# Encoder layers 0 to 4: the turned rows copied by VectorE, a new order of the steps, and new places for the last layer's end

## The chip, the core and the metric

The kernel runs on one NeuronCore of a Trainium2 chip. The metric is the device time of one execution in microseconds (us). Five engines work side by side, each through its own queue in order: PE (TensorE, matmuls; PEld is its weight loads), DVE (VectorE), ACT (ScalarE), POOL (GpSimd) and SP (SyncE, which here only issues DMAs). Engines wait for each other through semaphores.

## The reference, cut to what matters

Eight sequences of 256 rows with 128 features go through an encoder of six layers, a routed mixture of experts, a state-space block and two layers of local attention. The change touches the encoder's order, and the end of its last layer, where routing begins. One layer computes, for each sequence `h` (16 heads of 8, `rel` a fixed table that decays with the distance of two rows):

```python
q = (h @ wq.T + bq_).reshape(bh, sl, H, DH)
k = (h @ wk.T + bk_).reshape(bh, sl, H, DH)
scores = jnp.einsum('blhd,bmhd->bhlm', q, k) * inv_sqrt_d
w_avg = jax.nn.softmax(scores, axis=-1).mean(axis=1)
new_w = jax.nn.softmax(CSCALE * w_avg + rel[None], axis=-1)
sa = jnp.einsum('blm,bme->ble', new_w, h)
h1 = _ln(h + sa, l1w, l1b)
h2 = _ln(h1, l2w, l2b)
ff = jax.nn.relu(h2 @ w1.T + b1_) @ w2.T + b2_
return (_ln(h2 + ff, l3w, l3b), None)
```

After the six layers each row is normalized again and sent to one of eight experts; a shared expert takes every row.

## The kernel before, in words

**One block.** `plan(n, l, b)` (L450) lists the steps of one sequence b in one layer l; with six layers and eight sequences there are 48 such blocks, numbered n. Each step is a small function, and almost each belongs to one engine.

- `f_transpose` (PE, L463) turns the block's rows into `pt`; `f_copy` (ACT, L468) copies them to `ht`; `f_qk` (PE, L473 and L474) makes queries and keys in `pqk`; `f_bias` (DVE, L479 and L483) adds the biases and writes `qt`, `kt`; `f_mask` (POOL, L490) spreads the queries over masked copies `qm`.
- Scores come in four portions k of 64 rows and all 16 heads. `s_matmul k` (PE, L502) writes four tiles `s` of one PSUM bank each. For each of the four, `s_max k,g` (DVE, L512) takes the negated maxima and `s_exp k,g` (ACT, L516) two exponentials with their sums. `s_weights k` (DVE, L523) inverts the sums, `s_diag k` (POOL, L529) makes the diagonal weights `dg`.
- `mix c` (PE, L548, with the `rel` table at L546) adds the weighted heads of two portions up in `pacc`; `mix_exp c` (ACT, L558) is the second softmax's exponential, `nw`.
- `r_transpose` (PE, L567) and `r_copy` (DVE, L574) turn it; `r_mix` (PE, L581) applies it to the rows (`psa`); `r_add` (DVE, L590) adds the input and takes the first statistics (L426, L428); `rs1` and `r_norm1` (POOL: L274, L275, L444, L446, L280, L281) normalize to `t1`; `mv2` (DVE) takes the second statistics of `t1`, `rs2` and `r_norm2` (POOL) give `n2`, `r_residual` (POOL) `h2`.
- `r_transpose2` (PE, L615, `pt2`), `r_h2t` (DVE, L621), `r_ff10`, `r_ff11` (PE, L630, two `pf` tiles), `r_relu0` (ACT, L638), `r_relu1` (DVE, L640), `r_ff2` (PE, L646, `po`), `r_add3` (DVE, L654, with the third statistics), `rs3` and `r_norm3` (POOL) end the block.

**The order.** Nothing is scheduled by the compiler: each step has a place, in units of which a block has 16 (`SLOTS`), and block n starts at 16 n. All steps of all blocks are sorted by place and issued in that order, so each engine's queue is a weave of some six blocks in flight. The table `ORDER0` (L56) gives the places of layers 0 to 5; the last layer's sequences 3 to 7 have their own (`ORDER_END`, L74), its first three two changed entries (`LAST_NORM`, L188). `ORDER_ROUTE` (L152) places the routing of each sequence, `ORDER_SHARED` the shared expert, `BLOCKS` the routed experts' blocks.

```python
places = dict(ORDER0)
if l == DEPTH0 - 1 and b < 3:
    places.update(LAST_NORM)
elif l == DEPTH0 - 1:
    places = {name: at_b[b - 3] for name, at_b in ORDER_END.items()}
for name, fn, *args in steps:
    at(t0 + places[name], 0, lambda fn=fn, args=args: fn(*args))
```

**PSUM.** Six banks hold the `s` tiles (pool `ps_s`), so a portion of scores needs four banks that earlier exponentials have freed. The other two (pool `ps_m`) are shared by all else, ten tiles a block: `pt`, `pqk`, two `pacc`, `pnw`, `psa`, `pt2`, two `pf` and `po`. A tile's first matmul waits until the last reader of the bank's earlier tile is through.

**Around it.** `begin(b)` (L1029) normalizes the inputs of sequences 2 to 7 during the first blocks: statistics on DVE at place 3, the root on POOL at 5, the norm (L439) on DVE at 7. `state_space_weights` (L342) prepares weights for the later state-space block: on DVE a product over 128 x 1024 elements (L343), two copies of matmul results (L348), six small operations and eight fills, besides two matmuls, one exponential on ACT and one operation on POOL. It is issued once, at place 0.9 of block 8. In the last layer `route(b)` (L731) follows each sequence: norm, scores against the experts, choice, count, and two indirect DMAs on POOL (`send`, L825) that put the rows into the experts' buckets in HBM. `shared(q)` (L954) fits the shared expert in, and `block(j)` (L893) runs the 23 routed blocks after the last sequence.

Of the kernel before, what the change touches and what calls it, by code (L numbers as in the profile page):

```python
# [20 lines left out]
NB = 8  # L21
# [5 lines left out]
DEPTH0, HEADS0, DH0, FF0 = 6, 16, 8, 512  # L27
# [43 lines left out]
    "r_residual": 43.970, "r_ff2": 47.854, "r_add3": 50.870, "rs3": 59.957, "r_norm3": 73.951,  # L71
}

ORDER_END = {  # L74
    "f_transpose": (-22.588, -32.173, -31.874, -30.172, -34.750),
    "f_copy": (-21.688, -28.101, -28.555, -30.061, -31.562),
    "f_qk": (-15.007, -14.534, -23.086, -25.006, -11.950),
    "f_bias": (-11.801, -11.122, -22.761, -24.492, -11.386),
    "f_mask": (-6.524, -10.118, -9.553, -23.037, -10.705),
    "s_matmul0": (-1.917, -5.386, -4.976, -5.351, -2.724),  # L80
    "s_max0,1": (2.491, -1.850, -1.900, -1.396, -2.178),
    "s_max0,3": (-0.598, -2.685, -2.563, -4.623, -1.493),
    "s_max0,2": (2.064, -3.816, -1.374, 0.741, -0.178),
    "s_max0,0": (-0.500, -5.197, -3.092, -1.337, 0.111),
    "s_matmul1": (0.455, -4.912, -1.171, 0.708, 0.699),
    "s_max1,1": (3.047, -0.531, 1.568, 3.437, 2.386),
    "s_max1,3": (3.715, 2.999, 2.222, 2.638, 3.004),
    "s_max1,2": (3.231, -0.595, 2.205, 4.177, 3.024),
    "s_exp0,1": (3.643, -0.138, 0.483, -0.479, 4.027),
    "s_exp0,3": (0.851, -0.871, -0.805, 3.613, 4.500),  # L90
    "s_exp0,2": (3.180, -1.967, 1.421, 3.653, 5.676),
    "s_max1,0": (2.933, 0.569, 0.828, 3.343, 5.828),
    "s_exp0,0": (3.833, -2.528, -1.820, 1.700, 6.048),
    "s_matmul2": (5.225, 3.710, 1.519, 5.869, 6.113),
    "s_exp1,1": (4.254, 1.863, 1.976, 7.266, 6.121),
    "s_max2,2": (7.022, 4.300, 3.235, 9.812, 6.177),
    "s_max2,1": (5.683, 4.167, 4.387, 6.760, 6.819),
    "s_exp1,2": (6.460, 4.018, 2.497, 6.731, 7.639),
    "s_exp1,3": (5.773, 4.652, 2.319, 4.655, 7.897),
    "s_max2,3": (7.766, 5.905, 3.987, 7.528, 8.871),  # L100
    "s_exp1,0": (4.977, 3.283, 2.260, 7.101, 9.300),
    "s_max2,0": (6.315, 3.903, 3.011, 6.704, 9.322),
    "s_matmul3": (5.866, 5.622, 5.985, 7.454, 10.567),
    "s_exp2,3": (8.315, 8.107, 4.093, 9.815, 10.922),
    "s_exp2,2": (7.901, 7.763, 10.214, 10.035, 11.881),
    "s_weights1": (7.083, 6.767, 4.000, 9.885, 12.232),
    "s_weights0": (5.023, 2.985, 2.289, 7.492, 12.314),
    "s_exp2,0": (6.779, 5.030, 3.941, 7.395, 12.361),
    "s_exp2,1": (8.070, 7.574, 5.917, 8.060, 13.131),
    "s_max3,3": (8.729, 7.394, 11.437, 11.234, 13.794),  # L110
    "s_diag1": (9.827, 7.569, 7.357, 13.446, 14.625),
    "s_max3,2": (8.914, 10.690, 8.657, 10.503, 14.655),
    "s_weights2": (12.301, 15.947, 11.372, 12.768, 15.139),
    "s_diag0": (10.155, 11.733, 11.924, 12.185, 15.190),
    "s_exp3,3": (12.942, 10.368, 12.722, 13.062, 15.414),
    "s_max3,1": (7.821, 7.839, 7.230, 11.469, 16.156),
    "s_max3,0": (9.108, 7.588, 10.909, 12.174, 16.730),
    "mix0,0": (10.634, 12.537, 13.066, 14.510, 16.836),
# [12 lines left out]
    "r_copy": (24.987, 22.101, 26.159, 25.133, 25.460),
    "r_mix": (25.267, 24.231, 26.620, 26.265, 26.786),
    "r_add": (26.976, 25.221, 27.964, 26.481, 28.335),
    "rs1": (30.053, 28.735, 30.060, 27.687, 30.032),
    "r_norm1": (32.011, 30.898, 30.735, 32.891, 31.789),
    "mv2": (33.807, 32.685, 33.080, 34.231, 32.467),
    "rs2": (33.862, 34.167, 36.446, 35.913, 34.021),
    "r_norm2": (34.544, 36.241, 38.935, 36.012, 34.183),
    "r_transpose2": (37.022, 38.395, 39.134, 36.759, 35.411),
    "r_h2t": (38.682, 39.571, 40.982, 37.883, 36.035),  # L140
    "r_ff10": (42.293, 39.711, 42.076, 41.248, 36.086),
    "r_ff11": (44.071, 42.631, 44.347, 39.613, 36.743),
    "r_relu0": (43.173, 42.325, 44.133, 42.663, 37.228),
    "r_residual": (37.554, 45.597, 48.811, 47.127, 38.283),
    "r_relu1": (45.180, 45.140, 47.469, 41.160, 39.470),
    "r_ff2": (47.776, 52.122, 48.822, 44.199, 40.517),
    "r_add3": (49.717, 53.375, 50.144, 51.436, 41.812),
    "rs3": (52.100, 58.307, 50.265, 54.792, 43.345),
    "r_norm3": (52.128, 58.358, 53.988, 55.107, 43.817),
}  # L150

ORDER_ROUTE = {  # L152
    "stats": (57.612, 57.612, 57.612, 56.949, 58.400, 58.211, 56.128, 44.295),
    "scale": (60.894, 60.894, 60.894, 58.836, 58.984, 59.878, 56.249, 46.526),
    "norm": (62.335, 62.335, 62.335, 58.860, 62.344, 61.253, 58.677, 46.756),
    "turn": (62.504, 62.504, 62.504, 59.248, 63.854, 63.551, 59.091, 49.402),
    "turned": (63.254, 63.254, 63.254, 59.889, 67.055, 64.640, 59.917, 49.954),
    "score": (66.190, 66.190, 66.190, 64.538, 67.765, 66.095, 60.974, 51.586),
    "choose": (68.024, 68.024, 68.024, 65.682, 70.485, 70.473, 62.519, 51.710),
    "count": (68.716, 68.716, 68.716, 82.004, 71.716, 71.394, 64.683, 52.398),  # L160
    "decay": (70.616, 70.616, 70.616, 82.508, 71.081, 72.041, 63.836, 52.978),
    "gate": (76.085, 76.085, 76.085, 85.702, 78.182, 72.642, 64.451, 53.425),
    "weigh": (81.070, 81.070, 81.070, 86.757, 80.354, 73.182, 68.517, 54.034),
    "put": (70.108, 70.108, 70.108, 83.767, 80.866, 71.724, 67.600, 54.198),
    "send0": (83.835, 83.835, 83.835, 87.737, 83.795, 75.315, 69.536, 54.498),
    "send1": (83.933, 83.933, 83.933, 90.820, 87.761, 78.188, 69.998, 55.144),
}

ORDER_SHARED = {
    "up0": (12.819, 27.640, 35.497, 51.662),  # L170
    "up1": (33.023, 18.085, 43.056, 54.937),
    "up2": (55.700, 45.285, 35.385, 55.168),
    "silu0": (28.073, 32.749, 39.789, 55.600),
    "silu1": (33.768, 26.049, 45.482, 55.800),
    "silu2": (56.300, 55.400, 35.761, 55.900),
    "times1": (38.457, 42.862, 46.381, 56.000),
    "times0": (30.812, 34.798, 41.496, 56.600),
    "times2": (56.500, 56.100, 42.000, 56.800),
    "down0": (37.783, 56.200, 43.645, 57.100),
    "down1": (41.724, 57.000, 47.596, 57.200),  # L180
    "down2": (56.700, 57.300, 50.240, 57.600),
    "out": (56.900, 57.500, 55.500, 57.900),
    "turn": (57.400, 57.800, 56.400, 58.000),
    "add": (57.700, 58.100, 58.300, 58.200),
}

TABLE, REGISTERS, BLOCKS = 55.100, 55.200, 62.400
LAST_NORM = {"rs3": 51.325, "r_norm3": 53.252}  # L188


ORDER1 = {
# [56 lines left out]
def model_kernel(ctx: ExitStack, tc: tile.TileContext, A: dict, out: bass.AP):  # L248
    nc = tc.nc
# [111 lines left out]
    with ExitStack() as s0:  # L361
# [54 lines left out]
        SLOTS = 16  # L416
        slots = {}

        def at(slot, order, fn):
            slots.setdefault(round(slot + order / 10, 3), []).append(fn)  # L420
# [29 lines left out]
        def plan(n, l, b):  # L450
            t0 = SLOTS * n
            v = {}
# [12 lines left out]

            def f_copy():
                v["ht"] = wk.tile([P, T], F32, name="ht", tag="ht")
                nc.scalar.copy(v["ht"], v["pt"].rearrange("p n t -> p (n t)"))  # L468

            def f_qk():  # L470
                wa = v["w"][0]
# [213 lines left out]
                    steps += [(f"s_max{k},{g}", s_max, k, g), (f"s_exp{k},{g}", s_exp, k, g)]  # L685
            for c in range(NC):
                steps += [(f"mix{c},0", mix, c, 0), (f"mix{c},1", mix, c, 1), (f"mix_exp{c}", mix_exp, c)]
            places = dict(ORDER0)
            if l == DEPTH0 - 1 and b < 3:
                places.update(LAST_NORM)  # L690
            elif l == DEPTH0 - 1:
                places = {name: at_b[b - 3] for name, at_b in ORDER_END.items()}
            for name, fn, *args in steps:
# [317 lines left out]
            block(j, e1 + j)  # L1011
        at(e1 + 4, 9, where)

        at(SLOTS * NB, 9, lambda: state_space_weights(small_bank))
        for b in range(NB):
            at(
                SLOTS * (2 * NB + b) + 1, 0,
# [481 lines left out]
    with ExitStack() as s3:  # L1499
# [19 lines left out]
        SLOTS = 16  # L1519
# [346 lines left out]
        for n in range(DEPTH1 * NB):  # L1866
            l, b = n // NB, n % NB
# [114 lines left out]
```

## Time and profile before

| what | us |
|---|---|
| three runs | 1673.78, 1679.32, 1689.04; median 1679.32 |
| the profiled execution | 1682.49 |
| its span | 1680.6 |
| busy in the span: PE, DVE, ACT, POOL | 1527.3, 1411.0, 1287.0, 1184.7 |
| encoder layers 0 to 4, then the last layer to the routed experts | about 0 to 720, then to 910 |
| rest: routed experts, state space, local attention | 910 to 1680.6 |

The profiled execution is one of its own, 3.2 us above the median of the three runs; its span leaves out 1.9 us around the program. A line of a timeline gives the start and the length in us, the engine, the source line, the operation, the tile it writes and those it reads, their sizes and how many equal instructions were merged; in brackets the idle time before it and who ended it. A record can begin before its turn, while the one ahead of it is still running, so what an instruction takes of its queue is read from one start to the next. The grants of PE's clock stand as PEclk, 1.00 being full speed.

### The profile page before, as it was taken

Reading aid. Unit: us, or ns where it says so; the run is one execution under the profiler, and the core shown is the slowest. Engines: PE = TensorE matmul, PEld = TensorE weight load, DVE = VectorE, ACT = ScalarE, POOL = GpSimd, SP = SyncE. Lnnn points to the kernel's source line nnn. Section 1 sums busy time; section 2 is a strip of 40 time slices with the busy share of each in tenths; the row PEclk is TensorE's granted clock in tenths of the full one; section 3 lists DMA queues with packets and bytes.
Section 4 is the critical chain, followed back from the end, with each engine's and each line's share of the span. In section 5 each row is a group of like instructions: output and inputs, shape, how many; then the busy total and the mean of one; then the engine's idle time right before and its main releaser. Section 6 shows DMA issues by size and latency. Waiting matters only on the chain.

```text
span 1680.6 us, 37534 instructions
## 1 busy us (share of the span) xinstructions
PE 1527.3 (91%) x12864; PEld 918.9 (55%) x12880; DVE 1411.0 (84%) x3344; ACT 1287.0 (77%) x4593; POOL 1184.7 (70%) x1703
## 2 busy tenths in 40 slices
PE   7899999999999999999898868898986889999996
PEld 3565666666666666666664643232221555666664
DVE  5899899999999999998776437999897889888884
ACT  6898999999999999997661328775631677888873
POOL 3587888999888888888874026977864656666661
PEclk9999999999999999999899979999777999999997
DMA  4000064000000000000000320000000000000000
GB/s 116 2 2 2 18 205 139 18 12 2 4 27 2 2 19 11 2 2 1 8 8 21 111 56 11 1 0 1 1 0 1 1 2 1 1 2 1 8 7 13
DMA packets 43356, 35.36 MB, mean 21 GB/s; under 512 B 3973, under 2 KB 39327, under 8 KB 43167
## 3 DMA queue, kind: packets, MB, share of 16 engines
q1 hardware_dynamic: 40991, 30.10, 5.9%
q0 software_dynamic: 1024, 2.10, 0.4%
q8 instruction: 104, 1.70, 0.4%
q10 hardware_dynamic: 1152, 0.76, 0.2%
q14 instruction: 85, 0.70, 0.1%
HBM read 20.50 MB, written 12.45 MB: 20 GB/s over the span
## 4 chain that ended last, share of the span: by engine, by line
ACT 39%; PE 33%; DVE 20%; POOL 4%; issue 3%; DMA 1%; SPq 0%; DVEq 0%; POOLq 0%; ACTq 0%
ACT e L516 30%; PE s L502 4%; DVE h L1362 4%; PE pm L1444 3%; PE pacc L548 3%; PE pq L1586 2%; PE pm L1240 2%; DVE pm L1356 2%; ACT el L1693 2%; PE pe L913 2%; ACT r L638 1%; ACT nw L558 1%; PE sl L1670 1%; PE pte L1711 1%; DVE nm L1681 1%
## 5 line engine op out<-in xcount | busy, mean ns | idle before, releaser
L516 ACT ACTIVATE e<-s,nmax 128x256 f32<-128x256 f32 x1536 | 713.7, 498 | 39.0 <-DVE nmax L512 31.1
L512 DVE TENSOR_REDUCE nmax<-s 128x2 f32<-128x512 f32 x768 | 491.8, 677 | 69.8 <-PE s L502 65.1
L516 ACT ACTIVATION_READ_ACCUMULATOR e<-s,nmax 128x1 f32 x1536 | 354.1, 231 | 0.0
L502 PE MATMUL s<-kt,qm 32*128 32x256 f32 x3072 | 268.9, 413 | 8.7 <-ACT e L516 5.4
L502 PEld LDWEIGHTS s<-kt,qm 32*128 32x128 f32 x3072 | 160.7, 188 | 90.0 <-ACT e L516 56.2
L548 PE MATMUL pacc<-e,dg 128*32 128x256 f32 x3072 | 191.7, 390 | 2.2 <-DVE t L654 1.8
L1369 POOL TENSOR_TENSOR hc<-h,bc 128x1024 f32<-128x1024 f32 x64 | 150.4, 2356 | 60.2 <-DVE h L1362 55.7
L1362 DVE TENSOR_TENSOR_SCAN h<-da,pm 128x1024 f32<-128x1024 f32 x64 | 146.3, 2285 | 7.7
L1348 ACT ACTIVATE da<-pm,na 128x510 f32<-128x510 f32 x128 | 82.0, 682 | 86.5 <-PE pm L1444 86.0
L275 POOL TENSOR_TENSOR rs<-rs,mhalf 128x2 f32<-128x2 f32 x184 | 131.5, 715 | 15.3
L1693 ACT ACTIVATE el<-sl,nm,rn 128x128 f32<-128x128 f32 x256 | 114.4, 471 | 27.7 <-DVE nm L1684 27.7
L529 POOL TENSOR_TENSOR dg<-sel,z 128x256 f32<-128x256 f32 x192 | 116.3, 615 | 26.4 <-DVE z L523 25.4
L548 PEld LDWEIGHTS pacc<-e,dg 128*32 128x32 f32 x3072 | 91.4, 111 | 77.6 <-issue 18.2
L630 PE MATMUL pf<-h2t,wa 128*128 128x256 f32 x384 | 109.6, 409 | 24.7 <-DVE h2t L621 20.8
L1706 POOL TENSOR_TENSOR el<-el,rz 128x512 f32<-128x512 f32 x64 | 66.5, 1040 | 92.0 <-DVE rz L1701 92.0
L1444 PE MATMUL pm<-dt,ssel 32*128 32x512 f32 x256 | 114.3, 726 | 7.3 <-ACT da L1348 7.1
L274 POOL TENSOR_SCALAR rs<-mv 128x2 f32<-128x2 f32 x184 | 42.1, 229 | 111.5 <-DVE mv L428 49.3
L1444 PE MATMUL pm<-u,ssel 32*128 32x512 f32 x256 | 96.4, 751 | 17.4 <-DVE h L1362 17.4
L1586 PE MATMUL pq<-wqkv,y 128*128 128x512 f32 x192 | 98.3, 607 | 2.6 <-DVE hk L1541 1.8
L630 PEld LDWEIGHTS pf<-h2t,wa 128*128 128x128 f32 x384 | 66.6, 192 | 59.5 <-DVE h2t L621 31.0
L490 POOL TENSOR_TENSOR qm<-qt,kmask 128x1024 f32<-128x1024 f32 x48 | 90.9, 1893 | 8.7 <-DVE qt L479 8.7
L646 PE MATMUL po<-wf,r 128*128 128x128 f32 x768 | 95.5, 278 | 0.5 <-ACT xnt L759 0.5
(308 smaller groups left out, 3462.1 us busy)
## 6 DMA issues: line engine op xcount, KB each, us to landing
bucket<-zrow SPq DMA_DIRECT2D x1, 8640.0 KB, 28.8
ln<-in_ln_dram SPq DMA_DIRECT2D x6, 448.0 KB, 4.6
wa<-in_wa_dram SPq DMA_DIRECT2D x6, 384.0 KB, 3.0
wf<-in_wf_dram SPq DMA_DIRECT2D x6, 256.0 KB, 3.7
wqkv<-in_wqkv_dram SPq DMA_DIRECT2D x1, 1536.0 KB, 7.7
xb<-bucket SPq DMA_DIRECT2D x23, 64.0 KB, 1.8
routed<-ob SPq DMA_DIRECT2D x23, 64.0 KB, 1.6
w<-in_w1e_dram SPq DMA_DIRECT2D x1, 1408.0 KB, 32.4
```

Of the source, the lines that this page charges most:

```text
L275: nc.gpsimd.tensor_tensor(dst, dst, mhalf.to_broadcast(list(dst.shape)), ALU.pow)
L502: nc.tensor.matmul(ss[g][:, i, :], v["qm"][rows, 2 * k + i].rearrange("p j q -> p (j q)"), v["kt"][rows, :], start=True, stop=True,)
L512: nc.vector.tensor_reduce(v["nmax", k][:, g, :], v["s", k][g], AX.X, ALU.max, negate=True)
L516: nc.scalar.activation(v["e", k][:, g, i, :], v["s", k][g][:, i, :], AF.Exp, bias=v["nmax", k][:, g, i : i + 1], accum_out=v["z", k][:, g, ...
L529: nc.gpsimd.tensor_tensor(dg, sel32.unsqueeze(1).to_broadcast(sh), z.unsqueeze(2).to_broadcast(sh), ALU.mult)
L548: nc.tensor.matmul(acc, v["dg", k][:, 2 * g + i, :], v["e", k][:, g, i, :], start=(g == 0), stop=False,)
L630: nc.tensor.matmul(pf[:, i, :], v["w"][0][:, f0 : f0 + P], v["h2t"], start=True, stop=True)
L1362: nc.vector.tensor_tensor_scan(h.rearrange("p h t -> p (h t)"), da, pu.rearrange("p h t -> p (h t)"), 0.0, ALU.mult, ALU.add)
L1369: nc.gpsimd.tensor_tensor(hc, v["h", n], v["bc", 1].unsqueeze(1).to_broadcast([P, 2, T2]), ALU.mult)
L1444: nc.tensor.matmul(dst, ssel[rows, j, :], pairs[n // NU][src][rows, f, :], start=True, stop=True)
L1586: nc.tensor.matmul(pq, yb[:, col : col + P], wqkv[:, l, i * INNER : (i + 1) * INNER], start=True, stop=True)
L1693: nc.scalar.activation(v["e", c][:, par, j, :], v["s", c][par][:, j, :], AF.Exp, scale=v["rn", c][:, 0, h : h + 1], bias=v["nm", c][:, par ...
```

## The change

There are three parts. In layers 0 to 4 `f_copy` runs on VectorE; in layer 5 it stays on ScalarE. Layers 0 to 4 get their own table of places, `ORDER0_MID`; the first three sequences of the last layer keep `ORDER0`. All entries of `ORDER_END`, `ORDER_ROUTE` and `ORDER_SHARED` are new, and `state_space_weights` moves by half a block. No step is added or left out, and no tile changes.

On the queues the order of layers 0 to 4 becomes, with the block that holds scores k=0 to 3 (before | after, PE):

```
before: s0, f_transpose, r_ff2, s1, f_qk, mix1, s2, r_transpose2, r_transpose, r_ff10, r_ff11, s3, r_mix, mix0
after:  f_transpose, s0, r_ff2, s1, f_qk, mix1, r_transpose2, s2, r_transpose, r_ff10, r_ff11, s3, r_mix, mix0
```

And on DVE (max k,g written as k,g):

```
before: 0,0 0,1 0,3 0,2 weights3 r_add3 1,1 mv2 1,0 1,2 f_bias 1,3 2,0 r_h2t 2,3 r_copy weights0 2,2 2,1 weights1 r_relu1 3,0 3,2 3,3 weights2 r_add 3,1
after:  f_copy weights2 0,0 0,3 0,1 0,2 weights3 mv2 r_add3 1,0 1,1 f_bias 1,2 1,3 r_h2t 2,0 2,3 r_copy 2,1 weights0 weights1 2,2 r_relu1 3,0 3,3 3,2 r_add 3,1
```

The diff, cut to its core:

```diff
+ORDER0_MID = {
+    "f_transpose": -19.823, "f_copy": -18.774, "f_qk": -16.041, "f_bias": -13.573, "f_mask": -5.202,
+    "s_matmul0": -3.511, "s_max0,0": -2.123, "s_max0,3": -2.119, "s_max0,1": -1.547, "s_max0,2": -1.354,
+    "s_exp0,0": -0.956, "s_matmul1": -0.329, "s_exp0,3": -0.229, "s_exp0,1": 0.057, "s_exp0,2": 0.783,
+    "s_max1,0": 1.861, "s_exp1,0": 2.010, "s_max1,1": 2.262, "s_max1,2": 3.071, "s_max1,3": 3.166,
+    "s_matmul2": 3.424, "s_max2,0": 3.550, "s_exp1,1": 4.481, "s_max2,3": 4.524, "s_exp1,2": 6.360,
+    "s_exp1,3": 6.910, "s_exp2,0": 7.661, "s_exp2,3": 7.930, "s_max2,1": 8.553, "s_weights0": 8.771,
+    "s_weights1": 8.773, "s_max2,2": 8.913, "s_exp2,1": 8.978, "s_matmul3": 9.260, "s_exp2,2": 9.652,
+    "s_diag1": 9.824, "s_diag0": 9.969, "s_max3,0": 10.522, "s_max3,3": 11.463, "mix0,0": 11.481,
+    "s_max3,2": 11.760, "s_exp3,0": 11.917, "mix0,1": 11.918, "s_max3,1": 12.492, "s_exp3,3": 13.208,
+    "s_exp3,2": 13.397, "s_weights2": 13.510, "s_exp3,1": 14.143, "mix_exp0": 15.984,
+    "s_weights3": 16.899, "s_diag2": 16.920, "s_diag3": 17.112, "mix1,0": 17.265, "mix1,1": 18.451,
+    "mix_exp1": 21.223, "r_transpose": 21.311, "r_copy": 21.746, "r_mix": 27.022, "r_add": 27.833,
+    "rs1": 30.227, "r_norm1": 32.917, "mv2": 33.313, "rs2": 33.897, "r_norm2": 34.536,
+    "r_transpose2": 35.136, "r_h2t": 35.246, "r_residual": 37.075, "r_ff10": 39.619, "r_ff11": 39.804,
+    "r_relu0": 40.631, "r_relu1": 42.081, "r_ff2": 46.041, "r_add3": 49.357, "rs3": 51.402,
+    "r_norm3": 70.600,
+}
...
 ORDER_END = {
-    "f_transpose": (-22.588, -32.173, -31.874, -30.172, -34.750),
-    "f_copy": (-21.688, -28.101, -28.555, -30.061, -31.562),
...
+    "f_transpose": (-18.099, -32.959, -30.372, -44.313, -32.882),
+    "f_copy": (-15.749, -27.979, -28.300, -42.867, -31.983),
...
 ORDER_ROUTE = {
...
-    "send0": (83.835, 83.835, 83.835, 87.737, 83.795, 75.315, 69.536, 54.498),
-    "send1": (83.933, 83.933, 83.933, 90.820, 87.761, 78.188, 69.998, 55.144),
...
+    "send0": (84.560, 84.560, 84.560, 82.264, 85.177, 76.555, 68.103, 55.033),
+    "send1": (84.593, 84.593, 84.593, 86.272, 87.524, 79.139, 70.111, 55.058),
...
 ORDER_SHARED = {
-    "up0": (12.819, 27.640, 35.497, 51.662),
-    "up1": (33.023, 18.085, 43.056, 54.937),
...
+    "up2": (55.400, 41.040, 31.991, 52.251),
+    "silu2": (55.700, 44.065, 40.072, 53.643),
...
-TABLE, REGISTERS, BLOCKS = 55.100, 55.200, 62.400
-LAST_NORM = {"rs3": 51.325, "r_norm3": 53.252}
+TABLE, REGISTERS, BLOCKS = 55.100, 55.200, 62.600
+LAST_NORM = {"rs3": 51.325, "r_norm3": 53.276}
...
             def f_copy():
                 v["ht"] = wk.tile([P, T], F32, name="ht", tag="ht")
-                nc.scalar.copy(v["ht"], v["pt"].rearrange("p n t -> p (n t)"))
+
+                copy = nc.scalar.copy if l == DEPTH0 - 1 else nc.vector.tensor_copy
+                copy(v["ht"], v["pt"].rearrange("p n t -> p (n t)"))
...
-            places = dict(ORDER0)
+            places = dict(ORDER0 if l == DEPTH0 - 1 else ORDER0_MID)
             if l == DEPTH0 - 1 and b < 3:
                 places.update(LAST_NORM)
...
-        at(SLOTS * NB, 9, lambda: state_space_weights(small_bank))
+        at(SLOTS * NB + 8, 3, lambda: state_space_weights(small_bank))
```

## The prediction

> **What bounds the kernel now.** I read four views in this order: busy time by stage, the timeline of each engine over one block (one sequence of one layer), the waits, and the stage around the folded weights. Columns of the first: stretch, its length, then busy time and count of PE, PE's weight loads, DVE, ACT and POOL, granted clock, DMA share, GB/s.
>
> ```profile
> core 0: us, PE busy (x) PEld busy (x) DVE busy (x) ACT busy (x) POOL busy (x), PEclk, DMA share, GB/s
> 107.98:126.03 18.05, 16.48 (x183) 11.11 (x180) 17.32 (x49) 16.85 (x73) 15.58 (x29) 1.00 0.01 2
> 159.63:182.60 22.97, 19.98 (x187) 12.66 (x184) 19.45 (x62) 17.00 (x73) 18.20 (x33) 0.85 0.00 1
> 400.51:417.31 16.80, 16.31 (x183) 10.94 (x181) 15.55 (x44) 16.73 (x72) 15.28 (x28) 1.00 0.01 2
> 720.46:910.00 189.54, 171.63 (x1511) 115.13 (x1509) 155.71 (x500) 128.50 (x521) 149.15 (x275) 0.95 0.02 6
> ```
>
> The reader is to see: a steady block takes 16.80 us (so from copy to copy, all the way from 126 to 720 us), ACT is busy 16.73 of it, PE 16.31, DVE 15.55. Three engines are nearly full, so the sum of none decides; a loop through all of them does. It shows in the block's rows (start, length):
>
> ```profile
> 407.89 2.33 PE L630 MATMUL pf<-h2t,wa 128*128 128x256 f32 x8 [0.41 <-DVE h2t L621]
> ...
> 414.28 1.15 PE L502 MATMUL s<-kt,qm 32*128 32x256 f32 x16
> 415.36 0.44 PE L463 MATMUL pt<-ident,h 128*128 128x128 f32 x2
> 415.63 1.95 PE L646 MATMUL po<-wf,r 128*128 128x128 f32 x16
> 417.51 1.85 PE L502 MATMUL s<-kt,qm 32*128 32x256 f32 x16
> 419.29 0.70 PE L473 MATMUL pqk<-ht,wa 128*128 128x256 f32 x2
> ```
>
> ```profile
> 415.45 2.48 DVE L512 TENSOR_REDUCE nmax<-s 128x2 f32<-128x512 f32 x4 [0.48 <-PE s L502]
> 416.25 0.47 ACT L516 ACTIVATE e<-s,nmax 128x256 f32<-128x256 f32 x1
> 417.62 0.48 ACT L516 ACTIVATE e<-s,nmax 128x256 f32<-128x256 f32 x1
> 418.06 0.38 ACT L468 COPY ht<-pt 128x256 f32<-128x256 f32 x1
> 418.24 0.72 PEld L502 LDWEIGHTS s<-kt,qm 32*128 32x128 f32 x10 [0.42 <-ACT e L516]
> ```
>
> Scores k=0 start at 414.28; their first maximum starts 1.17 later (DVE waited for it), the first exponential 0.80 after that; two pairs of exponentials end at 418.10, 1.85 on, and free the last of the four banks that scores k=1 need; PE, which stood in that step for the bank, is through at 419.29, 1.19 later. Sum 5.01, of which PE fills 4.30 (k=0 1.08, pt 0.27, po 1.88, k=1 1.07): 0.71 us of slack lie there. From there PE runs from step to step (402.49 to 414.28): pqk 1.06, mix 1.98, k=2 1.07, pt2 0.28, pnw 0.60, **0.41 waiting for h2t**, pf 2.25, k=3 1.08, psa 1.09, mix 1.97: 11.79. 5.01 + 11.79 = 16.80, the whole block. So a step is worth something only where it stands on this loop. ACT's own work is 16 pairs x 0.893 + nw 0.72 + relu 0.71 + copy 0.26 = 15.98; the rest are restarts after short waits.
>
> **The copy.** It leaves ACT: one COPY takes 0.26 us of its queue (418.06 until the next start). That isn't on the loop: the copy stands behind exponential 0,1, which already freed the bank. On DVE the nearest row has the same shape and also reads PSUM:
>
> ```profile
> L348 DVE COPY wdt<-pk x2: 424/424/425, 161.0 to 162.2; 128x256 f32<-128x256 f32 x2
> ```
>
> 0.42 us, 0.35 of the queue (161.01 to 161.35). Take k=0's start as 0. In the new order DVE ends r_add at -0.34, max 3,1 at 0.26, the copy at 0.61, a reciprocal at 0.72, and the first maximum can't start before 1.17: 0.45 us of the present 0.48 wait cover it, and the cost is nothing. Without that cover: 40 x 0.35 = 14 us. As pt is now released by DVE, po takes its buffer, and pqk (not po) waits for mix_exp0; mix_exp0 ends at 1.97 + 1.78 + 0.36 = 4.11, pqk starts at 5.01: free.
>
> **The new order, on the loop.** (1) f_transpose moves ahead of k=0, out of the stretch with slack into the chain: **+0.27**. (2) pt2 and h2t move ahead of k=2 and its maxima: the 0.41 wait goes. (3) What is late next is pf's second half, which needs the bank that r_copy empties: from k=2's start, max 2,0 at 1.17, max 2,3 at 1.77, r_copy 2.37 to 3.05 (row 0.68), 0.06 to PE as from h2t now: 3.11. PE is there at 1.07 + 0.60 + 1.12 = 2.79: waits 0.32. (Today r_copy ends at 409.03, as pf's second half begins.) Loop: 16.80 + 0.27 - 0.41 + 0.32 = **16.98, +0.18 a block**.
>
> Off the loop: mv2 and r_add3 (0.61 + 1.04) now both stand before max 1,0, so exponential 1,0 starts 0.24 late on ACT; its pair and the next end at 7.94, and k=2, which needs that bank, is due on PE at 8.33. On POOL qm (1.89) ends 1.1 us before rs1 is due; dg for both mixes is 1.1 us early or more.
>
> Rule against row: the Trainium skill (Perfetto Trace Analysis) says the most-contended engine is the one with the highest occupancy, to be optimized first. By that, ACT (16.73 of 16.80) loses 0.26 a block and 40 blocks give -10.4 us; by the loop the copy gives nothing and the order costs. I take the loop, because its rows add up to the block to 0.01; the other value is the first rival.
>
> **Blocks with the first norms** (six, 18.05 us). They carry 1.78 us more DVE work (17.32 against 15.54): the norm, 1.33 for two L439 instructions, stands right before h2t and so in the loop. In the new order it stands behind r_copy, but with the copy DVE has 17.32 + 0.35 = 17.7 us of work, and becomes the bound: 17.8. 6 x -0.25 = -1.5 (from -5 to +2).
>
> **The folded weights** (state_space_weights, 22.97 - 16.80 = 6.17 now) move from behind scores k=1 to behind pf: every DVE instruction of it (3.97 us without waits), two matmuls, one exponential on ACT ahead of relu0, one on POOL. Its first matmul now waits for relu0, and queued behind it on DVE are max 2,1, max 2,2 and relu1, for which the mix waits: late by 3.97 + 1.3 of waits - 0.9 slack = 4.4, PE idle over 2 us. Now the clock:
>
> ```profile
> 162.50:165.00 2.50, 1.13 (x4) 0.68 (x4) 2.50 (x15) 0.26 (x1) 1.38 (x3) 0.79 0.00 0
> 165.00:167.50 2.50, 2.24 (x22) 1.31 (x26) 2.47 (x11) 2.50 (x12) 0.87 (x3) 0.50 0.00 0
> ```
>
> PE's longest wait there was 1.42 us, and yet the granted clock fell to 0.50 for some 5 us, and the mix took 4.00 instead of 1.93. The skill (TensorE: Matmul & The Clock Gate, Part 1) lets the clock halve after an idle window of about 3.4 us, which would spare the new place: 4.4 us in all, -1.8. By the row it halves again, +2.1: 6.5 in all. I take the row: +0.3 (-2 to +3).
>
> **The last layer** (189.5 us, of which 8 x 16.8 = 134 would be plain blocks). Here POOL is the queue to watch: 149 us busy, and its second send of each pair waits for the first one to land:
>
> ```profile
> 828.13 0.96 POOL L825 DMA_INDIRECT bucket<-xn,pos  x1 [3.06 <-DMA bucket<-xn,pos]
> ```
>
> Six such waits cost 10.7 us. The first three pairs stay adjacent in the new queue; the fourth gets two dg (1.19) between: -1.2. All sends, and their DMAs, stay one per half sequence; SP's loads keep their places but for the routed blocks', which follow BLOCKS by 0.2 of a place. The other moves change which of route, shared expert and block fills which hole; no row prices that, so I bound it by those 10.7 us on either side, and take nothing for it.
>
> **Sum.** 32 steady blocks (40 less the first, six with norms and one with the fold) x 0.18 = +5.8; -1.5; +0.3; -1.2: +3.4. The profiled execution took 1682.5 (span 1680.6, 1.9 around it), so 1685.9 for it; the median shown is 3.2 lower. **1683 us.**
>
> **Rivals.** (A) ACT sets the pace after all: for it speak the chain of waits (ACT 89% between 402 and 420) and that ACT, too, shows no wait there. 40 x 0.26 = 10.4: 1669; if the restarts close as well (0.82 a block), 40 x 1.08 = 43: 1636. Against: the 0.71 us that PE stands before a bank, and ACT's restarts, which wait for maxima that wait for PE. (B) Slower: mv2 now stands ahead of max 1,0 and waits for POOL's norm 1. r_add ends at -0.34, POOL needs 3.93 + 0.1 for rs1 and norm 1 (415.54 to 419.47): ready at 3.69, and DVE is there at 3.68. No margin. Max 1,0, exponentials 1,0 and 1,1 queue behind it; they have 0.4 us until k=2's bank is late, and from there each us counts. At 0.9 us late it costs 0.5 a block: 32 x 0.5 = 16: 1699. POOL has 1.1 us spare before rs1, so it must lose more than that in a block; that speaks against. (C) The middle is as forecast, and the last layer's places decide, by up to 10 us: 1673 or 1693.
>
> **Chances.** Forecast 0.50; A 0.22; B 0.16; C 0.12. This kernel's runs spread from 1673.8 to 1689.0, so under 1% can hardly be told from no change; 1% is below 1662.5 and above 1696.1. Of A, 0.16 lies below (the copy and a fifth of the restarts are enough), low ends of C and of the bounds add 0.03; of B 0.12 lies above, high ends add 0.05. Faster 0.19, same 0.64, slower 0.17. The range takes A down to 1659 and B up to 1700; the forecast's own is 1674 to 1692.
>
> **What would show it.** Right: blocks of about 17.0 us between 190 and 700; PE waiting some 0.3 for nwt before pf's second half and none for h2t; PE's stand in k=1 up from 0.42 to about 0.7; ACT idle about 0.7 before exponential 0,0. Wrong, towards A: blocks of 16.5 or less, with PE's stand in k=1 gone. Towards B: DVE waiting for t L281's writer before the second statistics. Towards C: equal blocks, and a stretch from the last plain block to the routed experts that isn't 189 us.

## The result and the profile after

| | before | after |
|---|---|---|
| median of the runs, us | 1679.32 | 1692.32 (1686.76 to 1698.14) |
| span of the profiled execution, us | 1680.6 | 1693.2 |
| ratio of the times | | 1.0085, 95% interval 1.0066 to 1.0104 |

The change makes the kernel 0.85% slower. The forecast was 1683; the sign is as forecast, and of the 13 us it had 3.4. The measured 1692.3 lies at the upper end of the forecast's own range, 1674 to 1692.

First the stages. In a steady block of after (columns as in the prediction: stretch, length, busy time and count of PE, weight loads, DVE, ACT, POOL, clock, DMA share, GB/s):

```profile
400.87:417.96 17.09, 16.39 (x182) 10.93 (x181) 15.98 (x44) 16.43 (x72) 15.35 (x27) 1.00 0.01 2
```

A block takes 17.09 us instead of 16.80. DVE has 0.43 more busy time, ACT 0.30 less, and the block got longer: the engine that was fullest was relieved, and that bought nothing. On the page of before, the chain that ended last and the exponentials:

```profile
ACT 39%; PE 33%; DVE 20%; POOL 4%; issue 3%; DMA 1%; SPq 0%; DVEq 0%; POOLq 0%; ACTq 0%
...
L516 ACT ACTIVATE e<-s,nmax 128x256 f32<-128x256 f32 x1536 | 713.7, 498 | 39.0 <-DVE nmax L512 31.1
```

On the page of after, the same two, and one group of PE:

```profile
PE 49%; DVE 26%; ACT 13%; POOL 7%; issue 3%; DMA 1%; ACTq 0%; SPq 0%; POOLq 0%; DVEq 0%
...
L537 ACT ACTIVATE e<-s,nmax 128x256 f32<-128x256 f32 x1536 | 708.4, 498 | 72.0 <-DVE nmax L533 59.4
...
L651 PE MATMUL pf<-h2t,wa 128*128 128x256 f32 x384 | 105.3, 399 | 23.8 <-DVE nwt L595 19.6
```

ACT's share of the chain falls from 39% to 13%, and the idle time before the exponentials grows from 39.0 to 72.0 us. ACT stands and waits more, so in after it does not set the pace. The last line names the new wait, for `nwt`, which `r_copy` writes. Both are seen in one block, first PE (start, length):

```profile
400.50 0.44 PE L482 MATMUL pt<-ident,h 128*128 128x128 f32 x2
400.87 1.15 PE L523 MATMUL s<-kt,qm 32*128 32x256 f32 x16
401.94 2.05 PE L667 MATMUL po<-wf,r 128*128 128x128 f32 x16
...
404.83 1.13 PE L523 MATMUL s<-kt,qm 32*128 32x256 f32 x10 [0.19 <-ACT e L537]
405.88 0.70 PE L494 MATMUL pqk<-ht,wa 128*128 128x256 f32 x2
...
410.85 1.03 PE L651 MATMUL pf<-h2t,wa 128*128 128x256 f32 x4
412.39 1.13 PE L651 MATMUL pf<-h2t,wa 128*128 128x256 f32 x4 [0.51 <-DVE nwt L595]
```

Then DVE and ACT, at the start of the same block:

```profile
401.03 0.41 DVE L489 COPY ht<-pt 128x256 f32<-128x256 f32 x1
402.03 2.48 DVE L533 TENSOR_REDUCE nmax<-s 128x2 f32<-128x512 f32 x4 [0.47 <-PE s L523]
```

```profile
402.84 0.47 ACT L537 ACTIVATE e<-s,nmax 128x256 f32<-128x256 f32 x1 [0.53 <-DVE nmax L533]
```

The reader is to see that from k=0 (400.87) to `pqk` (405.88) it is 5.01 us, exactly as before, although ACT no longer copies there. `pt` now stands ahead of that stretch and adds 0.37. The rest of PE's steps, with 0.51 of waiting for `nwt` in place of 0.41 for `h2t`, is 11.71. 5.01 + 0.37 + 11.71 = 17.09. (The line numbers of after are those of before plus 21.)

Where the 12.6 us of the spans arise is read from one landmark, the start of the second `mix_exp` of each block n, after minus before (one execution of each):

| stretch | difference, us | forecast |
|---|---|---|
| first two blocks | +3.0 | none |
| to n = 6, the blocks with the first norms | -1.9 | -1.5 |
| to n = 9, with the folded weights | -1.3 | +0.3, and 0.2 a block |
| to n = 38, 29 steady blocks | +8.4 | 29 x 0.18 = +5.2 |
| to n = 40, where the two tables meet | +4.6 | none |
| from there to the end | -0.2 | -1.2 |

The steady blocks explain two thirds. The first and the fifth row were not in the forecast at all. The last row says nothing of the new places: from n = 40 to the end, executions that keep the tail of before differ from it by -4.1 (e12) to +1.8 us (e4). This is PE where layer 4's blocks, in the new order, overlap those of layer 5, in the old one:

```profile
695.68 0.44 PE L482 MATMUL pt<-ident,h 128*128 128x128 f32 x2 [1.18 <-ACT nw L579]
...
703.16 1.99 PE L651 MATMUL pf<-h2t,wa 128*128 128x256 f32 x8 [0.53 <-DVE kt L504]
...
707.96 1.93 PE L569 MATMUL pacc<-e,dg 128*32 128x256 f32 x32 [0.64 <-POOL dg L550]
...
717.91 0.70 PE L494 MATMUL pqk<-ht,wa 128*128 128x256 f32 x2 [0.55 <-ACT nw L579]
```

None of these four waits is in a steady block of either order: 1.18 + 0.53 + 0.64 + 0.55 = 2.9 us of PE, besides the `nwt` wait. The other 1.7 of the 4.6 us are not laid to a wait here.

### The profile page after: what moved, and what is told of

It is laid out like the page before. It is cut to its first block, busy times and chain, and to the rows that moved or that the text cites. A ratio compares the mean times of both kernels' runs of the same rounds, so it can differ in the third digit from the quotient of the medians.

```text
span 1693.2 us, 37259 instructions
## 1 busy us (share of the span) xinstructions
PE 1535.3 (91%) x12864; PEld 919.1 (54%) x12880; DVE 1419.0 (84%) x3384; ACT 1275.1 (75%) x4553; POOL 1188.7 (70%) x1703
## 4 chain that ended last, share of the span: by engine, by line
PE 49%; DVE 26%; ACT 13%; POOL 7%; issue 3%; DMA 1%; ACTq 0%; SPq 0%; POOLq 0%; DVEq 0%
PE s L523 10%; PE pacc L569 8%; DVE nmax L533 6%; ACT e L537 6%; DVE h L1383 4%; PE pf L651 2%; PE pm L1465 2%; PE pq L1607 2%; PE psa L602 2%; DVE pm L1377 2%; PE pm L1261 2%; ACT el L1714 2%; PE pqk L494 1%; POOL rs L294 1%; PE pe L934 1%
## 5 line engine op out<-in xcount | busy, mean ns | idle before, releaser
L523 PE MATMUL s<-kt,qm 32*128 32x256 f32 x3072 | 274.0, 415 | 16.6 <-ACT e L537 12.7
L651 PE MATMUL pf<-h2t,wa 128*128 128x256 f32 x384 | 105.3, 399 | 23.8 <-DVE nwt L595 19.6
L1465 PE MATMUL pm<-dt,ssel 32*128 32x512 f32 x256 | 110.6, 707 | 7.3 <-ACT da L1369 6.3
L667 PEld LDWEIGHTS po<-wf,r 128*128 128x128 f32 x768 | 89.5, 191 | 15.4 <-DVE z L544 10.9
```

What stands on the lines that cost most here:

```text
L523: nc.tensor.matmul(ss[g][:, i, :], v["qm"][rows, 2 * k + i].rearrange("p j q -> p (j q)"), v["kt"][rows, :], start=True, stop=True,)
L651: nc.tensor.matmul(pf[:, i, :], v["w"][0][:, f0 : f0 + P], v["h2t"], start=True, stop=True)
L667: nc.tensor.matmul(po[:, c, :], v["r"][:, f, c * P : (c + 1) * P], v["w"][1][:, f, :], start=(f == 0), stop=(f == 3),)
L1465: nc.tensor.matmul(dst, ssel[rows, j, :], pairs[n // NU][src][rows, f, :], start=True, stop=True)
```

## The experiments

The theory, from the prediction: the block is a loop. PE runs its steps one after the other, then stands in k=1 until the chain k=0, first maximum, two pairs of exponentials has freed the banks. A step costs its own time where it lies in PE's part, and nothing where it lies beside that chain. The rivals: ACT's work sets the pace; DVE, with the copy, does; or the loss lies in the last layer.

### Which part carries the loss

**e1_mid_only**: after, with the last layer's tables of before (`ORDER_END`, `ORDER_ROUTE` and `ORDER_SHARED` whole, and these lines).

```diff
-TABLE, REGISTERS, BLOCKS = 55.100, 55.200, 62.600
-LAST_NORM = {"rs3": 51.325, "r_norm3": 53.276}
+TABLE, REGISTERS, BLOCKS = 55.100, 55.200, 62.400
+LAST_NORM = {"rs3": 51.325, "r_norm3": 53.252}
```

> Layers 0 to 4 as in the changed kernel (copy on VectorE, new table, weights folded at the new place), the last layer with its old places. Loop theory: steady blocks of 17.09 us as in the changed kernel, 33 of them 0.29 above 16.80, so +9.6; first blocks +1.3; fold -2.3: about +8.6, 1688. What the profile shows at the join of layers 4 and 5 (+4) goes to whichever part owns it: about 1692 if the join of the two tables makes it, 1688 if the last layer's new places do. Rival, the last layer's places are the whole loss: near 1679.

Measured: 1692.11, ratio 1.0081 (1.0053 to 1.0109). Blocks of 17.09; the block where the tables meet takes 22.13 instead of 16.8. The middle and this join are the whole loss.

**e2_tail_only**: the other half, before with the last layer's new tables alone (the same tables and lines the other way round).

```diff
-TABLE, REGISTERS, BLOCKS = 55.100, 55.200, 62.400
-LAST_NORM = {"rs3": 51.325, "r_norm3": 53.252}
+TABLE, REGISTERS, BLOCKS = 55.100, 55.200, 62.600
+LAST_NORM = {"rs3": 51.325, "r_norm3": 53.276}
```

> The kernel before with only the last layer's new places (all tables but the one of layers 0 to 4). Blocks of 16.80 in every theory. Loop theory: what is left of the loss beside layers 0 to 4, which is 14 - 8.6 = about +5 if the last layer's places own the join, +1 if not: 1680 to 1685. Rival, the last layer's places are the whole loss: +13, 1692.

Measured: 1680.62, ratio 1.0009 (0.999 to 1.0029). Blocks 16.80, and 16.80 at the join. The last layer's new places are worth nothing that can be measured, so rival C falls.

**e3_copy_only**: before, with the copy on VectorE at its old place. The folded weights are at their new place with it, since at the old one, by the order of the queues, DVE and PE would wait for each other (argued, not run).

```diff
-                nc.scalar.copy(v["ht"], v["pt"].rearrange("p n t -> p (n t)"))
+                copy = nc.scalar.copy if l == DEPTH0 - 1 else nc.vector.tensor_copy
+                copy(v["ht"], v["pt"].rearrange("p n t -> p (n t)"))
...
-        at(SLOTS * NB, 9, lambda: state_space_weights(small_bank))
+        at(SLOTS * NB + 8, 3, lambda: state_space_weights(small_bank))
```

> The kernel before with the copy on VectorE in layers 0 to 4 at its old place, and the weights folded at the new place, which that copy needs. Loop theory: the copy (0.35 of DVE's queue) falls between the last maximum of k=0 and the first of k=1, where ACT has 0.33 to spare: blocks of 16.8 to 16.9, 1677 to 1682. Rival, DVE's extra work is what costs: 17.15 a block, +0.35 x 40 = +14, 1693. Rival A, ACT paces: 16.54, 1669.

Measured: 1679.75, ratio 1.0008 (0.9986 to 1.003). A steady block of it:

```profile
397.56:414.36 16.80, 16.31 (x184) 10.94 (x180) 15.82 (x44) 16.59 (x71) 15.23 (x28) 1.00 0.01 1
```

It takes 16.80, as before (a few take 16.82): taking 0.26 us from ACT, which was busy 16.73 of 16.80, changes it by 0.00. The blocks with the first norms, where DVE is fullest, became longer, 18.4 instead of 18.05, so in those the copy is not free at its old place.

**e4_weights_only**: before, with only this.

```diff
-        at(SLOTS * NB, 9, lambda: state_space_weights(small_bank))
+        at(SLOTS * NB + 8, 3, lambda: state_space_weights(small_bank))
```

> The kernel before with only the folding of the state-space weights moved by half a block. By the profile of the changed kernel the stage around it is some 2.3 us cheaper there: 1677. By the row of the clock as predicted +0.3: 1680. Blocks elsewhere 16.80 in both.

Measured: 1676.32, ratio 0.9987 (0.997 to 1.0004); the stage 2.1 us shorter, all else equal. This part of the change is at worst harmless. The clock in it:

```profile
167.50:170.00 2.50, 1.95 (x8) 1.02 (x7) 2.50 (x3) 0.96 (x4) 2.50 (x1) 0.98 0.00 0
170.00:172.50 2.50, 2.50 (x19) 1.30 (x17) 2.50 (x18) 0.18 (x1) 2.23 (x6) 0.50 0.00 0
172.50:175.00 2.50, 2.50 (x26) 2.20 (x30) 2.50 (x7) 2.30 (x11) 2.33 (x5) 0.83 0.00 0
```

It falls to 0.50 here too, but for half as long as at the old place (3.41 us instead of 6.83). That stretch in e4, then in before:

```profile
169.92:173.33 3.41, 3.41 (x22) 2.13 (x21) 3.41 (x21) 1.01 (x5) 3.15 (x7) 0.50 0.00 0
```

```profile
163.95:170.78 6.83, 5.52 (x48) 3.19 (x52) 5.60 (x26) 5.98 (x26) 4.01 (x7) 0.50 0.00 0
```

**e5_order_only**: e1 with the copy on ScalarE in all layers, between exponentials 3,1 and 0,0.

```diff
-    "f_transpose": -19.823, "f_copy": -18.774, "f_qk": -16.041, "f_bias": -13.573, "f_mask": -5.202,
+    "f_transpose": -19.823, "f_copy": -17.050, "f_qk": -16.041, "f_bias": -13.573, "f_mask": -5.202,
...
-                copy = nc.scalar.copy if l == DEPTH0 - 1 else nc.vector.tensor_copy
-                copy(v["ht"], v["pt"].rearrange("p n t -> p (n t)"))
+                nc.scalar.copy(v["ht"], v["pt"].rearrange("p n t -> p (n t)"))
```

> As e1, but the copy stays on ScalarE in all layers, placed between exponentials 3,1 and 0,0, where ACT has 0.5 us idle in the changed kernel. Loop theory: the order alone makes the loss, blocks of 17.1 to 17.2, total as e1 (1692) or up to 4 above. Rival, the copy on VectorE makes it together with the order: blocks of 16.8, 1682.

Measured: 1693.67, ratio 1.0098 (1.0072 to 1.0123); blocks 17.09, the join 22.14:

```profile
402.11:419.20 17.09, 15.97 (x185) 10.84 (x181) 15.64 (x44) 16.70 (x72) 15.35 (x27) 1.00 0.01 2
```

With e3 this is a clean pair: in the steady blocks and at the join the order alone makes the whole loss, the engine of the copy none of it.

### Is it a loop through PE

**e9_before_norel**: before, with PE's work cut and nobody else's.

```diff
-                for g in ((0, 1), (2, 3, 4))[part]:
+                for g in ((0, 1), (2, 3))[part]:
...
-                        if g == 4:
-                            r0 = T - 32 - P * c - 32 * q
-                            nc.tensor.matmul(acc, selb, relb[:, r0 : r0 + T], start=False, stop=True)
```

> The kernel before, without the four matmuls of each mix that add the table of relative places (a bf16 quarter-row each, 0.22 us of PE's queue a mix); the second softmax lacks that term. Nothing is taken from ACT, DVE or POOL. If a loop through PE sets the block, as the forecast had it, both mixes stand on its PE stretch (the 11.79 us), so a plain block loses 2 x 0.22 = 0.44: 16.36 instead of 16.80, and the 39 blocks from the second to the fortieth some 17 us, with the last layer up to 20: about 1660. If a second loop lies close behind, it stops short of that, at 16.5 to 16.6 (1668 to 1672). If ACT sets the pace (16.73 us busy of 16.80, nothing taken from it), blocks stay at 16.8 and the time at 1679.

Measured: 1672.65, ratio 0.9961 (0.994 to 0.9982). One block of it, whole, and its PE rows:

```profile
500.49:517.07 16.58, 16.08 (x173) 10.69 (x173) 15.54 (x43) 16.56 (x73) 14.62 (x27) 1.00 0.01 2
```

```profile
501.55 1.93 PE L544 MATMUL pacc<-e,dg 128*32 128x256 f32 x32
503.41 1.15 PE L502 MATMUL s<-kt,qm 32*128 32x256 f32 x16
...
510.19 1.93 PE L544 MATMUL pacc<-e,dg 128*32 128x256 f32 x32
512.06 1.15 PE L502 MATMUL s<-kt,qm 32*128 32x256 f32 x16
...
517.07 0.70 PE L473 MATMUL pqk<-ht,wa 128*128 128x256 f32 x2
```

The mixes take 1.86 and 1.87 of PE's queue instead of 1.98 and 1.97: 0.22 less together. The expectation had 0.44, by reading the 0.22 from the `rel` record's start to the next step as its cost; half of it is the tail of the mix itself. The block is 0.22 shorter, and from k=0 (512.06) to `pqk` (517.07) it still is 5.01. So what PE saves in its part of the loop the block saves in full, while ACT's work is untouched and its busy time just shrinks with the block (16.56 of 16.58). e3 took work from ACT and got nothing; this took work from PE and got all of it. (16.58 is also where the expectation put a second loop, but the rows show no new wait: `h2t` is waited for 0.41 as before. In eight blocks, n = 15 to 22, one mix took up to 0.2 longer again, and the block 16.67 to 16.78; why is not shown.)

### The two terms of the loop, one by one

**e6_pt_late**: e1 with `pt` behind k=0, in the slack, and the copy behind the first maximum of k=0.

```diff
-    "f_transpose": -19.823, "f_copy": -18.774, "f_qk": -16.041, "f_bias": -13.573, "f_mask": -5.202,
+    "f_transpose": -19.500, "f_copy": -18.121, "f_qk": -16.041, "f_bias": -13.573, "f_mask": -5.202,
```

> As e1, but f_transpose comes behind scores k=0 again, with the copy on VectorE right behind the first maximum of k=0. Loop theory: pt (0.37 of PE) leaves the chain, po waits for the copy and sends k=1 through 0.16 later: 17.09 - 0.37 + 0.16 = 16.88 a block, 33 x -0.21 = -7 against e1: 1685. If f_transpose's place is not what costs: 17.09 or more.

Measured: 1688.56, ratio 1.0054 (1.003 to 1.0077); blocks 17.00, not 16.88. PE:

```profile
414.89 1.18 PE L523 MATMUL s<-kt,qm 32*128 32x256 f32 x16
...
417.13 2.05 PE L667 MATMUL po<-wf,r 128*128 128x128 f32 x16 [0.69 <-DVE ht L489]
419.11 1.15 PE L523 MATMUL s<-kt,qm 32*128 32x256 f32 x16
```

`pt` did leave the chain (-0.37). But with two banks for all tiles but the scores, `po` takes the bank that the copy empties, and stands 0.69 for it: from k=0 to `pqk` it is 5.30 instead of 5.01. -0.37 + 0.29 = -0.08, and the block lost 0.09.

**e7_rcopy_early**: e1 with `r_copy` ahead of the second maximum of k=2, so that `pf` need not wait.

```diff
-    "s_matmul2": 3.424, "s_max2,0": 3.550, "s_exp1,1": 4.481, "s_max2,3": 4.524, "s_exp1,2": 6.360,
+    "s_matmul2": 3.424, "s_max2,0": 3.550, "s_exp1,1": 4.481, "s_max2,3": 5.800, "s_exp1,2": 6.360,
```

> As e1, but r_copy comes ahead of maximum 2,3 on VectorE. Loop theory: PE's 0.51 us wait for nwt before the second half of pf goes; exponential 2,3 gets its maximum 0.3 later, and scores k=3 wait some 0.25 for its bank: 16.85 a block, -0.24 x 33 = -8 against e1: 1684. If the wait for nwt is off the path: 17.09.

Measured: 1698.44, ratio 1.0104 (1.005 to 1.0158); blocks 17.19, not 16.85. PE:

```profile
414.11 2.08 PE L651 MATMUL pf<-h2t,wa 128*128 128x256 f32 x8
416.12 1.84 PE L523 MATMUL s<-kt,qm 32*128 32x256 f32 x16
417.89 1.16 PE L602 MATMUL psa<-h,nwt 128*128 128x128 f32 x8
```

The wait is gone (one row of eight), and k=3 takes 1.77 until `psa` starts, where it took 1.08: the maximum that was put back lets its exponentials start late, and k=3 stands for their bank. PE came 0.51 earlier to k=3, the maximum came 0.60 later, and 0.69 of standing is left: the second loop had some 0.4 us to spare.

**e8_both**: e6 and e7 together, both diffs.

> e6 and e7 together. Loop theory: the two stand at different places of one loop and add up: 17.09 - 0.21 - 0.24 = 16.64 a block, 1677; ACT's own work (15.72 without restarts) leaves room for it. If another loop (ACT through its restarts) comes next: blocks stop at 16.8.

Measured: 1694.81, ratio 1.0095 (1.0066 to 1.0123); blocks 17.14. Both waits are there again: `po` stands 0.52 for `ht`, and k=3 takes 1.77. No kernel with the new order came below 17.00 a block: each of these reorders met another wait at once.

**e10_mixexp_early** and **e11_mixexp_rcopy**: a try to pass the next one. Both are e5 (copy on ACT) with the first mix's exponential and the copy in the gap ahead of exponential 0,0; e11 has e7's edit as well.

```diff
-    "f_transpose": -19.823, "f_copy": -17.050, "f_qk": -16.041, "f_bias": -13.573, "f_mask": -5.202,
+    "f_transpose": -19.500, "f_copy": -16.960, "f_qk": -16.041, "f_bias": -13.573, "f_mask": -5.202,
...
-    "s_exp3,2": 13.397, "s_weights2": 13.510, "s_exp3,1": 14.143, "mix_exp0": 15.984,
+    "s_exp3,2": 13.397, "s_weights2": 13.510, "s_exp3,1": 14.143, "mix_exp0": 15.030,
```

> The new order of layers 0 to 4 with the old tables for the last layer and the copy on ACT, and three places changed: the first mix's exponential in the gap in which ACT waits for the first maximum of k=0 (before it stood behind exponentials 0,0 and 0,3), the two transposes of the turned rows behind k=0 instead of ahead of it, the copy right behind that exponential. By the loop: pt leaves the chain (-0.37) and po waits neither for the copy nor for the exponential, since both end before it is due; k=0 to k=1 stays 5.01; a block 17.09 - 0.37 = 16.72. The exponential's 0.36 also leaves ACT's queue between exponentials 0,3 and 2,3. The two tables still meet at layer 5: +5 there. First blocks as after. So 1692 - 34 x 0.37 = 1679. If the order's loss lies elsewhere (DVE or POOL), blocks stay at 17.0 to 17.1: 1691.

> The same with the second maximum of k=2 behind r_copy, so that the 0.5 us wait of pf's second half goes; in the earlier run with that change alone another loop (exponential 2,3 late, its bank, k=3) took it back and more. Here exponential 2,3 has 0.36 us more room, as the first mix's exponential no longer stands ahead of it. If that loop is what was met, a block falls below 16.72, to 16.72 - 0.5 + (0.7 - 0.36) = about 16.55 or less, down to 16.3 (PE's own work); the time 1672 to 1668 with the +5 where the tables meet. If not, 16.8 as in the earlier run less 0.37: 1682.

Measured: e10 1690.84, ratio 1.0094 (1.006 to 1.0128), blocks 17.06; e11 1701.4, ratio 1.0151 (1.0123 to 1.0178), blocks 17.42. ACT of e10 around k=0 (which starts at 417.26), then PE:

```profile
418.39 0.57 ACT L536 ACTIVATE e<-s,nmax 128x256 f32<-128x256 f32 x1
418.84 0.49 ACT L578 ACTIVATE nw<-pacc 128x256 f32<-128x256 f32 x1
419.19 0.48 ACT L488 COPY ht<-pt 128x256 f32<-128x256 f32 x1
419.44 0.61 ACT L536 ACTIVATE e<-s,nmax 128x256 f32<-128x256 f32 x1
```

```profile
419.47 0.71 PE L666 MATMUL po<-wf,r 128*128 128x128 f32 x4 [0.69 <-ACT nw L578]
```

The expectation let `nw` end long before `po` is due. But ACT's 0.53 of idle time begins only when the exponentials of k=3 are through: `nw` starts 1.58 after k=0, `po` waits 0.69 for its bank, and exponential 0,0 starts 2.18 after k=0 instead of 1.97. In e10 PE's chain therefore passes through ACT's `nw`. e11 has the same wait (0.70) and e7's as well (k=3 takes 1.77). Both are misses, and they show that a gap has a place in time and not only a size.

### The version that beats both

In after, the six blocks with the first norms were shorter than before. **e12_weights_norm** takes that and e4's part alone: before, with the folded weights at their new place and the norms of `begin` behind `r_copy`.

```diff
             for k, fn in enumerate(begin(b)):
-                at(t0 + 2 * k, 0, fn)
+                at(t0 + (0, 2, 5.4)[k], 0, fn)
...
-        at(SLOTS * NB, 9, lambda: state_space_weights(small_bank))
+        at(SLOTS * NB + 8, 3, lambda: state_space_weights(small_bank))
```

> The kernel before with the folded weights at their new place (alone: 1676.3, the stage 2.2 us shorter) and the first norms of layer 0 (two L439 instructions of 0.67 us on DVE, in six blocks) behind r_copy instead of ahead of h2t, which is where the new order has them; order, copy and last layer as before. By the loop: h2t no longer waits for 1.33 us of norm, of which r_copy, maxima and k=3 behind it can give back half; after's blocks of this kind took 17.45 where before took 18.05, so 6 x -0.6 = -3.6 us beside the -2.2: about 1673, ratio 0.9965. If the norm is only moved from one place of DVE's full queue to another (DVE 17.32 us busy in these blocks), blocks stay at 18.05 and the time at 1676.

Measured: 1673.61, ratio 0.9954 (0.9933 to 0.9975); by n = 9 it is 5.8 us ahead (3.4 by the norms, 2.2 by the folded weights), and it keeps that through the encoder. `pf` in a block with norms, first of before, then, with the whole block, of e12:

```profile
115.86 2.33 PE L630 MATMUL pf<-h2t,wa 128*128 128x256 f32 x8 [1.49 <-DVE h2t L621]
```

```profile
104.20:121.19 16.99, 16.46 (x183) 11.10 (x182) 16.47 (x49) 16.74 (x72) 15.64 (x29) 1.00 0.01 2
```

```profile
112.02 2.33 PE L630 MATMUL pf<-h2t,wa 128*128 128x256 f32 x8 [0.41 <-DVE h2t L621]
```

The norm is off the loop: the wait falls by 1.08, the block from 18.05 to 16.99, with the same instructions. The norm itself became shorter, too. POOL and DVE of before, then DVE of e12:

```profile
113.12 1.89 POOL L490 TENSOR_TENSOR qm<-qt,kmask 128x1024 f32<-128x1024 f32 x1
114.02 1.33 DVE L439 TENSOR_SCALAR h<-x,mv,rs 128x128 f32<-128x128 f32 x2
```

```profile
113.14 0.58 DVE L439 TENSOR_SCALAR h<-x,mv,rs 128x128 f32<-128x128 f32 x2
```

At the old place the first of the two instructions takes 1.08 us instead of 0.34 and ends just behind POOL's `qm` (115.01); so it is in three of the six blocks. At the new place none of them meets `qm`, and none is stretched. So two useful parts of the change were hidden in it, under the cost of its order.

## Why the prediction was right, and where its sizes were off

**The frame held.** It took the loop against the rule of the Trainium skill (Perfetto Trace Analysis, Identifying the Most-Contended Engine) that the engine with the highest occupancy comes first. By that rule the copy's removal is worth 10 us; e3 shows 0.00 a block and a ratio of 1.0008, and e9 the reverse side: 0.22 off PE, 0.22 off the block. In this case the rule names the wrong engine, because all three are nearly full and wait for each other in turn.

**The copy** at nothing: right. DVE still waits 0.47 for k=0's maxima with the copy ahead of them (forecast: 0.45 of the present 0.48 cover it).

**The new order, on the loop**: right in each step, small in size. The 5.01 stayed 5.01; the wait for `h2t` went; `pf`'s second half starts 3.10 after k=2 (forecast 3.11), and its wait took over. That wait is 0.51 and not 0.32, but this costs nothing: PE comes 0.20 earlier (2.59 after k=2, not 2.79, since `pnw` and half of `pf` take 0.49 and 1.03, where the forecast took 0.60 and 1.12 from rows with other neighbours), and goes on when the forecast said. The mis-sized terms are the two transposes: `pt` 0.37 for 0.27, and `pt2` 0.37 for 0.28, which the forecast left as it was. Less 0.08 behind k=2, that is the 0.11 between +0.29 a block and +0.18: 3.2 us over 29 blocks. Two of the forecast's signs came smaller than it said: PE's weight loads stand 0.59 in k=1 (forecast about 0.7), and ACT is idle 0.53 before exponential 0,0 (forecast about 0.7).

**The join of the two tables** is the term missing from the sum. The prediction gave the last layer's boundary to "the other moves" and took nothing for it; it weighed the moves inside the last layer, and not that blocks of two orders run woven together for some two blocks. From n = 38 to 40 it costs 4.5 to 6.0 us in every kernel with two tables (the longest block there 20.5 to 22.1 in after, e1, e5 to e8, e10 and e11) and nothing in those with one (16.8 in e2, e3, e4 and e12).

**The first blocks**, +3.0, were left out of the sum as well. They come with the new order: e1 has +3.4 and e5 +3.1, while e2, e3, e4 and e12, with the old one, have -0.5 to +1.4. (e9 has +2.6 with the old order, but there PE's clock was at half for twice as long as in before.) Which wait makes them was not tried.

**The first norms**: direction right, reason wrong. DVE was not to become the bound at 17.7: of the 17.32 us of busy time in the row, 0.74 is the norm's first instruction standing until POOL's `qm` ends, and not work. e12 has the same 49 instructions in 16.47 us.

**The folded weights**: +0.3 forecast; -1.3 in after, -2.1 in e4. Here the row (the clock fell at waits of 1.42) was weighed against the rule (TensorE: Matmul & The Clock Gate, Part 1: an idle window of about 3.4 us). The clock did fall, as the row said, in before, after, e1 and e4, and ahead of the fall no wait of PE in the stage was longer than 0.6 us: here no idle window of that length was needed for it, and the measurement decides. In before, too, the fall (at 163.95) comes as the wait of 1.42 begins, behind waits of 0.55 and 0.52, so that wait can hardly be its cause. But how long it lasts differs from execution to execution of the same code. After, then e1, then the same stretch of e12, whose stage is that of e4:

```profile
172.83:176.24 3.41, 3.41 (x22) 2.44 (x20) 3.41 (x19) 1.82 (x8) 1.52 (x3) 0.50 0.03 7
```

```profile
173.70:180.53 6.83, 6.53 (x48) 3.89 (x46) 6.04 (x26) 5.51 (x23) 4.17 (x6) 0.50 0.00 1
```

```profile
163.90:174.20 10.30, 8.30 (x85) 5.46 (x86) 10.23 (x35) 6.24 (x27) 9.74 (x14) 1.00 0.01 2
```

In e12 it did not fall at all. In e1, whose stage is the same as after's, it caught the mix (3.64 us), as the forecast had it, and the stretch to n = 9 came to +0.3 (forecast 0.3 + 3 x 0.18 = +0.8); in after it was over when the mix began (1.93), and the same stretch came to -1.3. First e1, then after:

```profile
176.39 3.64 PE L569 MATMUL pacc<-e,dg 128*32 128x256 f32 x32 [0.30 <-DVE r L661]
```

```profile
176.19 1.93 PE L569 MATMUL pacc<-e,dg 128*32 128x256 f32 x32
```

What the stage costs beyond plain blocks of its own kernel is 4.0 us in e4 and after (half clock for 3.41 us) and in e12 (none), and 5.6 in e1 (6.83). The forecast had 4.4 without a fall and 6.5 with one. Its 4.4 for DVE's queue was nearly right; its 2.1 for the clock held only where the fall lasted into the mix. A shorter one costs nothing: where PE is not slow, the mix waits for DVE instead (1.45 us in e12).

**The rivals.** A (ACT sets the pace) is refuted by e3, and by e9, where ACT's work stayed and the block became shorter. B (`mv2` waits for POOL and holds up max 1,0) did not come about: in the block shown POOL has `t` ready at 404.57, and `mv2` starts at 404.60. There is no margin, as forecast, but in 29 steady blocks DVE never waits there. C is refuted by e2; that its 1693 is close to the measured time is chance.

**The time as a whole.** The forecast's own way, the steady blocks, gave 8.4 of the 12.6 us. The first blocks and the join gave 7.6 that had no term in the sum, and the norms and the folded weights won back 3.2. That the change is slower follows from the loop; that it is slower by 0.85% and not by 0.2% comes more from the two missing terms than from the mis-sized one.

## What to carry to other kernels

Where several engines are nearly full, take the block apart into the loop of waits that closes on itself, check that its rows add up to the period, and price an edit only by what it adds to or takes from that loop; then ask for the next loop, which in e7 lay within 0.4 us. When part of a pipelined program gets a new order, price the boundary too: where blocks of two orders overlap, neither order's balance holds. And test the parts of a change apart, since gains of 2.2 and 3.4 us were in it.

## What the runs showed of the hardware

- A pair of 128 x 128 transposes took 0.27 of PE's queue ahead of `po` and 0.28 ahead of `pnw`, but 0.37 ahead of a score step with its 32-row tiles, in the steady blocks of after. What a step costs depends on what follows it.
- In the stage of the folded weights PE's clock fell to 0.50 with no wait of PE over 0.6 us ahead of it (waits of 0.4 to 0.6 us follow each other there). It stayed there for 3.41 us (after, e4) or 6.83 us (before, e1), and in e12, with the same waits and one of 1.45 us behind them, it did not fall. What decides this is not shown.
- The same DVE instruction took 0.34 us, or 1.08 where POOL's `qm` ran, ending with it (before, three blocks). So the same 49 instructions were 17.32 us of DVE's busy time in before and 16.47 in e12: busy time is no fixed amount of work, and no floor for a block. What makes DVE stand there is not shown.
